# Seeding a PSUM bank from VectorE: beta1 h + bias is written ahead of the matmuls of z, in blocks 11 to 22 of a sparse gated graph layer

## The chip, the cores and the metric

The kernel runs on one core of a Trainium2 chip. The metric is device time in microseconds. Before the change the median of three runs is 1075.63 us (1071.70 to 1077.29).

## The reference, cut to what matters

For 16 batches of 1024 nodes with 256 features, an adjacency of 1024 x 1024 with few non-zeros per column, and gates from a two-layer network:

```python
pre_u = einsum('bud,dk->buk', h, W1[:d]);  pre_v = einsum('bvd,dk->bvk', h, W1[d:])
hidden = relu(pre_u[:, :, None, :] + pre_v[:, None, :, :] + b1)
S = sigmoid(einsum('buvk,ko->buvo', hidden, W2)[..., 0] + b2[0])
a_t = einsum('buv,bud->bvd', S * A, h)
m_t = einsum('uv,bud->bvd', A, h) * h
z = beta1 * h + beta2 * (a_t @ Wa + ba) + beta3 * (m_t @ Wm + bm)
```

The last line is the one that the change touches. The kernel scales Wa by beta2 and Wm by beta3 once, and keeps `bias` = beta2 ba + beta3 bm as one row, so that z = beta1 h + bias + a_t Wa + m_t Wm.

## The kernel before, in words

**Blocks and steps.** The output is cut into 32 blocks: a group `g` of four batches and a tile `vt` of 128 target nodes. A block k takes ten steps, n = 10 k + s with s from 0 to 9. A step handles 128 edge slots. GpSimd gathers for them the rows `fetched` (source features and their products with W1) from a table in DRAM, up to eight steps ahead. TensorE spreads the targets' part over the slots (`expand`, L615, into the tile `pc`, two of them), VectorE adds it (`add`, L648), then does relu, the product with W2 and the sum over features in one instruction for each batch (`gate`, L656, four in a step). ScalarE takes the sigmoid (L659) and scales the left operands with it (L661), and TensorE aggregates (L673) into two accumulators, for two steps at a time, in odd steps.

**Work around the steps.** Spread over the ten steps of block k, written out by hand in `products(n, k, s)`, are:
- `rows` (L445 with w_u, then L461 on ScalarE): products for the table of a later group, in the range around the change at s = 2 and s = 8, up to step 222;
- `halves` (s = 1 and 3): the product with w_v for the next block, in two halves. Each takes a bank, starts with a row of b1 (`add_row`, L449), has eight matmuls (L445), and is read by ScalarE twice, into `X` (L482) and `low` (L483). VectorE then subtracts `X` from `low` (L484);
- `turn_over` (s = 8, 9, then 0 and 2 of the next block): four transposes (L691) of the copied accumulator `ev` (L681), a copy into `LT` (L694), and a product with h on VectorE (L705);
- `block_end` (s = 4 to 7, for the block before): z in two halves h = 0, 1 of two batches each. A half starts with the row of bias (`add_row`, L449), has eight matmuls with w_a and eight with w_m (L722), is copied out of PSUM by ScalarE (L736), and has beta1 h added by VectorE one step later (L737), which leaves z in `h_blk`. A DMA from SP's queue writes it (L739). In the last eight blocks, a matmul with beta1 times the identity takes the place of the addition for h = 1 (L726, L728).

**Order.** All engines' instructions stand in the program in the order in which this loop issues them; an engine runs its own in that order. `after(step, f)` puts work off to the end of a later step, behind that step's `gate`.

**The two small banks.** `small()` hands out the PSUM banks for rows, halves, transposes and z: a pool of two (`psm`), taken in turn. Who takes a bank waits until its last reader is done, which is ScalarE's copy. From s = 3 the turn is: half 1 of `halves` (bank X), z's first half (Y), z's second half (X), rows at s = 8 (Y), transposes (X), and so on.

`LISTS` is step 110 and `LAST` step 230. The lists of edges that need VectorE and GpSimd (`lists`, with the tile `few`, L335, L338) are made before step 110.

Of the kernel before, what the change touches and what calls it, by code (L numbers as in the profile page):

```python
# [7 lines left out]
FP = mybir.dt.float32  # L8
FR = mybir.dt.float32r
I32 = mybir.dt.int32  # L10
AF = mybir.ActivationFunctionType
ALU = mybir.AluOpType
AX = mybir.AxisListType
P = 128
# [3 lines left out]
def kernel(  # L18
# [42 lines left out]
    nc = tc.nc  # L61
    B, N, D = x.shape
    NT = N // P
    DC = D // P
    GB = 4
    NG = B // GB
# [4 lines left out]
    E = TW * P  # L71
# [17 lines left out]
    def load_rows(src, n, name, engine=nc.scalar, at_=None):  # L89
        t = const.tile([P, n], FP, name=name) if at_ is None else at_  # L90
        engine.dma_start(t, bass.AP(tensor=src.tensor, offset=src.offset, ap=[[0, P], [1, n]]))
        return t
# [8 lines left out]
    def fixed(shape, name, dt=FP):  # L101
        return const.tile(shape, dt, name=name)
# [9 lines left out]
    upto = fixed([P, E], "upto")  # L112
# [3 lines left out]
    row = rows32[:, 0:1]  # L116
# [62 lines left out]
    slot, nth = upto, upto[:, :S]  # L179


    unit = fixed([P, P], "unit", FR)
    nc.vector.tensor_scalar(unit, upto[:, :P], 0.0, None, ALU.is_ge)
    edge = fixed([P, 1], "edge")
    nc.vector.tensor_scalar(edge, inw, 0.0, None, ALU.is_equal)

# [6 lines left out]
    bias_p = fixed([P, D], "bias_p", FR)  # L193
# [12 lines left out]
    main = ctx.enter_context(ExitStack())  # L206
# [6 lines left out]
    lst = ExitStack()  # L213
    lists_done = lst.close
    lst = lst.enter_context(tc.tile_pool(name="lst", bufs=1))
    psc = main.enter_context(tc.tile_pool(name="psc", bufs=2, space=bass.MemoryType.PSUM))
    psa = main.enter_context(tc.tile_pool(name="psa", bufs=1, space=bass.MemoryType.PSUM))
    psm = main.enter_context(tc.tile_pool(name="psm", bufs=2, space=bass.MemoryType.PSUM))

    def small(name):  # L220
        return psm.tile([P, 512], FP, name="misc")


    def aside(vt):
# [17 lines left out]
    def lists(vt):  # L242
# [7 lines left out]
        for c in range(0, N, N if vt < EARLY else N // 2):  # L250
            c = slice(c, c + (N if vt < EARLY else N // 2))
# [36 lines left out]
        for i in range(4):  # L288
            nc.tensor.matmul(pw[:, i:i + 1], sums[:, i].rearrange("p w q v -> p (w q v)"), R[:, 0:1],
                             start=True, stop=True)  # L290
# [36 lines left out]
        nc.vector.tensor_tensor(thr[:, vt:vt + 1], last, none, ALU.add)  # L327
        yield "op"
        RR = lst.tile([P, NW, RC], FP, name="RR", bufs=2)
        few = lst.tile([P, E], mybir.dt.uint8, name="few", bufs=2)  # L330
        yield "slot"
        for w, mine in enumerate((soon, late)):
            nc.vector.tensor_scalar(RR[:, w, :], R, mine, None, ALU.mult)
# [68 lines left out]
    def after(step, f):  # L402
        due.setdefault(step, []).append(f)
# [41 lines left out]
                nc.tensor.matmul(p[:, bb * D:(bb + 1) * D], hT[:, 2 * h + bb, i, :], wt[:, i, :],  # L445
                                 start=(i == 0 and not begun), stop=(i == DC - 1), skip_group_check=begun)

    def add_row(p, parts):
        nc.tensor.matmul(p, unit, parts.unsqueeze(1).to_broadcast([P, 2, D]),  # L449
                         start=True, stop=False, skip_group_check=True)  # L450

    def rows(k, tab=None):

# [14 lines left out]

    cuts = {}

    def halves(k):
        X = cuts[k] = big.tile([P, NW, GD], FR, name="X")
        low = one.tile([P, GD], FP, name="low")
        for h in range(2):
            step = yield
            c = slice(2 * h * D, (2 * h + 2) * D)
            p = small("p")
            add_row(p, b1_p)  # L480
            half_product(p, hTs[order[k]], w_v, h, True)
            nc.scalar.copy(X[:, 0, c], p)  # L482
            nc.scalar.copy(low[:, c], p)  # L483
        after(step + (2 if k else 1), lambda: nc.vector.tensor_tensor(low, low, X[:, 0, :].bitcast(FP), ALU.subtract))  # L484
        yield
        nc.scalar.copy(X[W:, 1, :], X[W:, 0, :].bitcast(FP))
        for w in range(NW):
            yield
            nc.scalar.copy(X[(1 - w) * W:(2 - w) * W, w, :], low[w * W:(w + 1) * W])  # L489
# [46 lines left out]
    spare = spare_.rearrange("p b c n -> p b (c n)")  # L536
# [9 lines left out]
    marks, pcs, accs, evs, hbs, LTs, lefts = {}, {}, {}, {}, {}, {}, {}  # L546
# [12 lines left out]
    parts = halves(0)  # L559
    for t, turns_ in enumerate(script):  # L560
        step = t - 100
# [148 lines left out]
    def block_end(k):  # L710

        g, vt = order[k]
        hb = hbs[k]
        for h in range(2):
            for i, wt in ((1, w_a), (0, w_m)):
                step = yield
                if i:
                    pz = small("pz")
                    add_row(pz, bias_p)
                for bb in range(2):  # L720
                    for c in range(DC):
                        nc.tensor.matmul(pz[:, bb * D:(bb + 1) * D], LTs[k][:, 2 * h + bb, i if bb else 1 - i, c, :], wt[:, c, :],  # L722
                                         start=False, stop=(i == 0 and c == DC - 1), skip_group_check=True)
            if h == 1 and g == NG - 1:
                for bb in range(2):
                    nc.tensor.matmul(pz[:, bb * D:(bb + 1) * D], be1_eye[0], hb[h][:, bb, :], start=False, stop=True,  # L726
                                     skip_group_check=True)
                nc.scalar.copy(hb[h], pz.rearrange("p (b d) -> p b d", b=2))  # L728
                b = g * GB + 2 * h
                after(step + 2, lambda hb=hb[h], b=b: nc.sync.dma_start(  # L730
                    out[b:b + 2, vt * P:(vt + 1) * P, :].rearrange("b p d -> p b d"), hb))
                continue
            z = pz.rearrange("p (b d) -> p b d", b=2)
            if step >= ROOM:
                z = LTs[k][:, 2 * h].rearrange("p k c n -> p (k c n)").rearrange("p (b d) -> p b d", b=2)
                nc.scalar.copy(z, pz.rearrange("p (b d) -> p b d", b=2))  # L736
            after(step + 1, lambda hb=hb[h], z=z: nc.vector.scalar_tensor_tensor(hb, hb, be1, z, ALU.mult, ALU.add))  # L737
            b = g * GB + 2 * h
            after(step + 2, lambda hb=hb[h], b=b: nc.sync.dma_start(  # L739
                out[b:b + 2, vt * P:(vt + 1) * P, :].rearrange("b p d -> p b d"), hb))  # L740
        del hbs[k], LTs[k]
# [120 lines left out]
    ROOM, MORE, LISTS = 10, 3, 110  # L862
    LAST = (BS - NT - 1) * T
# [18 lines left out]
    for n in range(total + 2):  # L882
        k, s = divmod(n, T)
        if n < total - 3:
            last_in = n - 1 if n % 2 or n < ROOM else done
        else:
            last_in = n
        while done < min(last_in, total):
            gather_in(done)
            done += 1  # L890
        if n % TW == 1 and n // TW + 1 < total // TW:
            load_mark(n // TW + 1)
        if n < LAST:
            expand(n + 2)
            if n >= ROOM:
                fill(n, False)
            products(n, k, s)
        if n + 1 < total:
            add(n + 1)
        if n < total:  # L900
            gate(n)
            if n + 1 < total:
                left_adj(n + 1)
        do(n)
        if s == 8 and ROOM <= n < LAST:
            turn_over(k, 0, 0, n)
        if n >= LAST and n + 2 < total:
            expand(n + 2)
        if n == 1:
            bias = load_rows(bm, D, "bias", nc.sync, spare[:, 1])  # L910
            ba_b = load_rows(ba, D, "ba_b", nc.sync, spare[:, 2])
            be1 = load_rows(beta1, 1, "be1", nc.sync)
            be2 = load_rows(beta2, 1, "be2", nc.sync)
            be3 = load_rows(beta3, 1, "be3", nc.sync)
            after(10, scale_late)
        if s in (5, 7) and k < BS - 1:
            h = s // 7
            hb = big.tile([P, 2, D], FP, name="h_blk", bufs=4)
            hbs.setdefault(k, []).append(hb)
            g, vt = order[k]  # L920
            nc.sync.dma_start(hb.rearrange("p b d -> p (b d)"),
                              table[g][vt * P:(vt + 1) * P, GD + 2 * h * D:GD + (2 * h + 2) * D])
        if n == total - 6:
            hbs[BS - 1] = hT_free.pop(0).rearrange("p b c n -> p b (c n)")
            for v, m, f in tails:
                for h, o in tail_rows(x, v, m, f):
                    nc.sync.dma_start(h, o)
        for i in advance.get(n, ()):
            next(made[i], None)
        if n in start_list:  # L930
            running.append([made[start_list[n]], True, n])
            piece_of(running[-1], n)
        if n < ROOM or n >= LAST:
            fill(n, False)
        if n >= LAST:
            products(n, k, s)
        if n == LISTS:
            assert not running and all(next(x, None) is None for x in made)
            lists_done()
            more = main.enter_context(tc.tile_pool(name="more", bufs=1))  # L940
            hT_free.extend(hT_places(more, MORE, NH))
            be1_eye.append(more.tile([P, P], FP, name="be1_eye"))
            nc.vector.tensor_scalar(be1_eye[0], ident, be1, None, ALU.mult)
        if n == 120:
            nc.gpsimd.partition_all_reduce(longest, rest, P, bass_isa.ReduceOp.max)
            after(n + 12, count_rest)
# [115 lines left out]
```

## Time and profile before

| | before |
|---|---|
| median of three runs | 1075.63 us (1071.70 to 1077.29) |
| the profiled execution | 1082.24 us, its span 1080.4 us |
| TensorE (PE) busy | 1020.1 us (94%) |
| VectorE (DVE) busy | 1017.6 us (94%) |
| ScalarE (ACT) busy | 862.6 us (80%) |
| GpSimd (POOL) busy | 459.3 us (43%) |
| granted TensorE clock | 0.99 in the mean |
| row of bias or b1 (L449) | 126 matmuls, 411 ns (b1) and 397 ns (bias) each |
| beta1 h added by VectorE (L737) | 55 instructions, 744 ns each |

How to read it: a time in the profile is that of one instruction from its start to its end. Neighbouring instructions of one engine overlap at their ends, so what an instruction takes of its engine is the distance from its start to the next one's start. PE and PEld are TensorE's matmuls and its weight loads; a load runs beside the matmul before it.

### The profile page before, as it was taken

How to read it: one execution, taken by the hardware profiler on the slowest of the kernel's cores; microseconds unless marked ns; L12 is line 12 of the kernel's file. 1: busy time of each engine (PE TensorE's matmuls, PEld its weight loads, DVE VectorE, ACT ScalarE, POOL GpSimd, SP SyncE). 2: the span in 40 equal slices, each digit the busy share in tenths (PEclk: the TensorE clock that was granted, in tenths of full speed). 3: DMA queues.
4: the chain of work that ended last, by engine and by line, in shares of the span. 5: the costliest groups of instructions: out<-in, count | busy, mean ns of one | idle time of the engine just before them, and what ended most of it. 6: DMA issues, size and time to landing. Idle time of an engine off the chain costs nothing.

```text
span 1080.4 us, 24120 instructions
## 1 busy us (share of the span) xinstructions
PE 1020.1 (94%) x7673; PEld 731.3 (68%) x7673; DVE 1017.6 (94%) x3481; ACT 862.6 (80%) x2616; POOL 459.3 (43%) x456
## 2 busy tenths in 40 slices
PE   7777999999999999999999999999999999999996
PEld 6654676776666776677777767777766667666654
DVE  8687999998999999999999999999999999999993
ACT  3246787788888887898888888889889889999983
POOL 2666676555257334553333334333333333333330
PEclk9989999999999999999999999999999999999999
DMA  9999899999999999999999999999999999999991
GB/s 283 327 340 385 313 339 381 362 382 378 403 352 371 408 381 385 379 403 395 404 393 399 412 384 392 408 396 389 381 361 370 369 348 368 365 381 369 365 341 44
DMA packets 147752, 394.56 MB, mean 365 GB/s; under 512 B 18224, under 2 KB 94512, under 8 KB 111408
## 3 DMA queue, kind: packets, MB, share of 16 engines
q0 software_dynamic: 50544, 301.16, 70.9%
q1 hardware_dynamic: 83776, 78.66, 22.9%
q10 hardware_dynamic: 13296, 13.11, 3.5%
q8 instruction: 63, 1.03, 0.4%
q14 instruction: 73, 0.60, 0.1%
HBM read 396.93 MB, written 50.33 MB: 414 GB/s over the span
## 4 chain that ended last, share of the span: by engine, by line
PE 40%; DVE 34%; issue 10%; ACT 8%; DMA 5%; POOL 2%; another core or an unknown queue 0%; POOLq 0%; DVEq 0%; ACTq 0%
DVE fetched L656 16%; DVE fetched L648 12%; PE acc L673 10%; PE misc L722 10%; PE misc L445 9%; PE pc L615 7%; DMA fetched<-table,uidx 3%; PE misc L691 2%; ACT left L661 2%; DVE LT L705 1%; ACT X L489 1%; PE misc L449 1%; DVE low L484 1%; DVE h_blk L737 1%; DMA hT__635<-in_xT_dram 1%
## 5 line engine op out<-in xcount | busy, mean ns | idle before, releaser
L518 POOL DMA_INDIRECT fetched<-table,uidx x320 | 339.4, 1061 | 529.0 <-PE acc L673 389.0
L656 DVE SCALAR_TENSOR_TENSOR fetched<-fetched,w_b 128x256 f32<-128x256 f32 x1280 | 478.0, 419 | 0.0
L648 DVE TENSOR_TENSOR fetched<-fetched,pc 128x1024 f32<-128x1024 f32 x320 | 387.7, 1212 | 29.9 <-PE pc L615 19.4
L661 ACT ACTIVATE left<-left,gt 128x32 f32<-128x32 f32 (+1 forms) x1280 | 299.6, 305 | 10.4
L673 PE MATMUL acc<-fetched,left 128*32 128x256 f32 x4096 | 273.4, 385 | 6.3 <-ACT gt L659 3.7
L615 PE MATMUL pc<-X,mark 128*128 128x512 f32 x640 | 243.7, 462 | 10.9 <-DVE fetched L648 9.3
L673 PEld LDWEIGHTS acc<-fetched,left 128*32 128x32 f32 x4096 | 127.6, 109 | 112.1 <-issue 29.1
L615 PEld LDWEIGHTS pc<-X,mark 128*128 128x128 f32 x640 | 105.4, 189 | 88.9 <-issue 41.6
L659 ACT ACTIVATE gt<-sc,b_b 128x4 f32<-128x4 f32 x320 | 95.9, 300 | 46.7 <-DVE fetched L656 37.5
L722 PE MATMUL misc<-w_m,LT 128*128 128x256 f32 x496 | 117.3, 379 | 0.0
L722 PE MATMUL misc<-w_a,LT 128*128 128x256 f32 x496 | 117.2, 379 | 0.0
L445 PE MATMUL misc<-w_v,hT 128*128 128x256 f32 x448 | 107.6, 383 | 0.0
L722 PEld LDWEIGHTS misc<-w_a,LT 128*128 128x128 f32 x496 | 93.8, 189 | 15.3 <-issue 0.4
L722 PEld LDWEIGHTS misc<-w_m,LT 128*128 128x128 f32 x496 | 93.8, 190 | 15.1
L625 ACT ACTIVATE left<-onehot,val 128x64 f32<-128x64 bf16 (+1 forms) x320 | 102.9, 322 | 0.0
L385 POOL DMA_INDIRECT val<-in_adjT_dram,vidx x80 | 87.2, 1090 | 34.4 <-issue 20.4
L656 DVE DVE_READ_ACCUMULATOR fetched<-fetched,w_b 128x1 f32 x1280 | 100.7, 79 | 0.0
L691 PE MATMUL misc<-ident,ev 128*128 128x128 f32 x512 | 79.5, 278 | 18.5 <-issue 7.0
L445 PEld LDWEIGHTS misc<-w_v,hT 128*128 128x128 f32 x448 | 86.4, 193 | 14.3
L691 PEld LDWEIGHTS misc<-ident,ev 128*128 128x128 f32 x512 | 60.7, 141 | 45.7 <-ACT ev L681 15.2
L482 ACT CAST X<-misc 128x512 fp32r<-128x512 f32 x64 | 37.1, 580 | 55.2 <-PE misc L445 48.0
L445 PE MATMUL misc<-w_u,hT 128*128 128x256 f32 x320 | 76.6, 386 | 4.0 <-issue 3.8
(185 smaller groups left out, 1011.3 us busy)
## 6 DMA issues: line engine op xcount, KB each, us to landing
h_blk<-table SPq DMA_DIRECT2D x62, 256.0 KB
out_dram<-h_blk SPq DMA_DIRECT2D x62, 256.0 KB
hT<-in_xT_dram SPq DMA_DIRECT2D x28, 512.0 KB
table<-in_x_dram ACTq DMA_DIRECT2D x24, 512.0 KB
table<-tab SPq DMA_DIRECT2D x48, 256.0 KB
fetched<-table,uidx POOLq DMA_INDIRECT x320
table<-in_x_dram SPq DMA_DIRECT2D x8, 512.0 KB
table<-fetched SPq DMA_DIRECT2D x8, 512.0 KB
```

The source lines that it names most:

```text
L385: nc.gpsimd.indirect_dma_start(out=val[:, i, j:j + 1], out_offset=None, in_=adj_flat, in_offset=bass.IndirectOffsetOnAxis(ap=vidx[:, i, j: ...
L445: nc.tensor.matmul(p[:, bb * D:(bb + 1) * D], hT[:, 2 * h + bb, i, :], wt[:, i, :], start=(i == 0 and not begun), stop=(i == DC - 1), skip ...
L518: nc.gpsimd.indirect_dma_start(out=fetched[at_slot[n]], out_offset=None, in_=table[g], in_offset=bass.IndirectOffsetOnAxis(ap=uidx[:, vt * ...
L615: nc.tensor.matmul(pcs[n][:, c], marks[n // TW][:, j * P:(j + 1) * P], cuts[k][:, w, c], start=True, stop=True)
L625: nc.scalar.activation(lefts[n][:, :m, 1::GB, :], onehot[:, i, o:o + m, :].unsqueeze(2).to_broadcast([P, m, GB // 2, V]), AF.Copy, scale=v ...
L648: nc.vector.tensor_tensor(t, t, pcs.pop(n), ALU.add)
L656: nc.vector.scalar_tensor_tensor(t[:, b, :], t[:, b, :], 0.0, w2_b, ALU.max, ALU.mult, accum_out=sc[:, b:b + 1])
L659: nc.scalar.activation(gt, sc, AF.Sigmoid, bias=b2_b)
L661: nc.scalar.activation(lefts[n][:, :m, 2 * b, :], lefts[n][:, :m, 1 + b // 2 * GB, :], AF.Copy, scale=gt[:, b:b + 1])
L673: nc.tensor.matmul(accs[h][b * 2 * V:(b + 1) * 2 * V, r, :], left[:, i, 2 * b - b % 2:2 * b - b % 2 + 2].rearrange("p k v -> p (k v)"), f[ ...
L691: nc.tensor.transpose(pt[:, r, :, c, :], ev[:, r, c * P:(c + 1) * P], ident)
L722: nc.tensor.matmul(pz[:, bb * D:(bb + 1) * D], LTs[k][:, 2 * h + bb, i if bb else 1 - i, c, :], wt[:, c, :], start=False, stop=(i == 0 and ...
```

## The change

For the second half of z (h = 1) of the block that ends during blocks 11 to 22 (steps 113 to 223 carry the call), the bank is claimed earlier and filled by VectorE:

- At s = 3, right after ScalarE's two copies of `halves`' second half, `seed_z` claims the same bank X again. At the end of step s = 4 VectorE writes beta1 h + bias into it.
- At s = 6 `block_end` takes this bank instead of a new one and leaves out the row of bias. Its matmuls add to what is there.
- At s = 7 ScalarE copies the bank into `h_blk` itself, and the addition on VectorE at the end of s = 8 is gone.
- While the bank is kept, `small()` gives out only the other one. The pool of two tiles becomes two named tiles, one each.

Three more edits make room in SBUF for a `bias` that stays: `unit`, the 128 x 128 ones that are the weights of every row of bias or b1, becomes one column read with a step of zero; `few` has one buffer instead of two; `bias` has a tile of its own. The branches for steps from LAST on are not reached, since the call is limited to steps between LISTS and LAST.

```diff
-    unit = fixed([P, P], "unit", FR)
-    nc.vector.tensor_scalar(unit, upto[:, :P], 0.0, None, ALU.is_ge)
+    unit_ = fixed([P, 1], "unit", FR)
+    nc.vector.tensor_scalar(unit_, row, 0.0, None, ALU.is_ge)
+    unit = unit_.to_broadcast([P, P])
...
-    def small(name):
-        return psm.tile([P, 512], FP, name="misc")
+    turn_of, kept = [0], []
+
+    def small(name, bank=None):
+        if bank is None:
+            bank = turn_of[0] = 1 - turn_of[0]
+            if kept and kept[0][0] == bank:
+                bank = turn_of[0] = 1 - bank
+        return psm.tile([P, 512], FP, name=f"misc{bank}")
...
-        few = lst.tile([P, E], mybir.dt.uint8, name="few", bufs=2)
+        few = lst.tile([P, E], mybir.dt.uint8, name="few", bufs=1)
...
-    def add_row(p, parts):
+    def add_row(p, parts, start=True):
         nc.tensor.matmul(p, unit, parts.unsqueeze(1).to_broadcast([P, 2, D]),
-                         start=True, stop=False, skip_group_check=True)
+                         start=start, stop=False, skip_group_check=True)
...
+    def seed_z(k, step):
+        bank = turn_of[0]
+        pz = small("pz", bank)
+        kept.append((bank, pz))
+
+        def write():
+            z, hb = pz.rearrange("p (b d) -> p b d", d=D), hbs[k][1]
+            if step >= LAST:
+                nc.scalar.activation(z, hb, AF.Copy, scale=be1)
+            else:
+                nc.vector.scalar_tensor_tensor(z, hb, be1, bias.unsqueeze(1).to_broadcast([P, 2, D]), ALU.mult, ALU.add)
+        if step >= LAST:
+            write()
+        else:
+            after(step + 1, write)
...
             nc.scalar.copy(low[:, c], p)
+            if h == 1 and k > 1 and (LISTS < step < LAST):
+                seed_z(k - 2, step)
...
                 if i:
-                    pz = small("pz")
-                    add_row(pz, bias_p)
+                    filled = h == 1 and kept
+                    pz = kept.pop()[1] if filled else small("pz")
+                    if not filled or step >= LAST + 6:
+                        add_row(pz, bias_p, not filled)
...
-            if h == 1 and g == NG - 1:
+            by_eye = g == NG - 1 and h == 1
+            if by_eye:
...
+            if by_eye or filled:
                 nc.scalar.copy(hb[h], pz.rearrange("p (b d) -> p b d", b=2))
...
-            z = pz.rearrange("p (b d) -> p b d", b=2)
-            if step >= ROOM:
-                z = LTs[k][:, 2 * h].rearrange("p k c n -> p (k c n)").rearrange("p (b d) -> p b d", b=2)
-                nc.scalar.copy(z, pz.rearrange("p (b d) -> p b d", b=2))
-            after(step + 1, lambda hb=hb[h], z=z: nc.vector.scalar_tensor_tensor(hb, hb, be1, z, ALU.mult, ALU.add))
-            b = g * GB + 2 * h
+            else:
+                z = pz.rearrange("p (b d) -> p b d", b=2)
+                if step >= ROOM:
+                    z = LTs[k][:, 2 * h].rearrange("p k c n -> p (k c n)").rearrange("p (b d) -> p b d", b=2)
+                    nc.scalar.copy(z, pz.rearrange("p (b d) -> p b d", b=2))
+                after(step + 1, lambda hb=hb[h], z=z: nc.vector.scalar_tensor_tensor(hb, hb, be1, z, ALU.mult, ALU.add))
...
-            bias = load_rows(bm, D, "bias", nc.sync, spare[:, 1])
+            bias = load_rows(bm, D, "bias", nc.sync)
```

More of the change, by code (lines that the diff above doesn't have):

```diff
@@ L217 @@
     psa = main.enter_context(tc.tile_pool(name="psa", bufs=1, space=bass.MemoryType.PSUM))
-    psm = main.enter_context(tc.tile_pool(name="psm", bufs=2, space=bass.MemoryType.PSUM))
-    def small(name):
-        return psm.tile([P, 512], FP, name="misc")
+    psm = main.enter_context(tc.tile_pool(name="psm", bufs=1, space=bass.MemoryType.PSUM))
+    turn_of, kept = [0], []
[5 more added lines that the diff above has]
+        return psm.tile([P, 512], FP, name=f"misc{bank}")
     def aside(vt):
@@ L727, in block_end @@
                                      skip_group_check=True)
+            b = g * GB + 2 * h
+            if by_eye or filled:
                 nc.scalar.copy(hb[h], pz.rearrange("p (b d) -> p b d", b=2))
-                b = g * GB + 2 * h
-                after(step + 2, lambda hb=hb[h], b=b: nc.sync.dma_start(
-                    out[b:b + 2, vt * P:(vt + 1) * P, :].rearrange("b p d -> p b d"), hb))
-                continue
-            z = pz.rearrange("p (b d) -> p b d", b=2)
-            if step >= ROOM:
-                z = LTs[k][:, 2 * h].rearrange("p k c n -> p (k c n)").rearrange("p (b d) -> p b d", b=2)
-                nc.scalar.copy(z, pz.rearrange("p (b d) -> p b d", b=2))
-            after(step + 1, lambda hb=hb[h], z=z: nc.vector.scalar_tensor_tensor(hb, hb, be1, z, ALU.mult, ALU.add))
-            b = g * GB + 2 * h
+            else:
[4 more added lines that the diff above has]
+                after(step + 1, lambda hb=hb[h], z=z: nc.vector.scalar_tensor_tensor(hb, hb, be1, z, ALU.mult, ALU.add))
             after(step + 2, lambda hb=hb[h], b=b: nc.sync.dma_start(
```

## The prediction, made before the changed kernel ran

> **What bounds the kernel now.** I read the page first, then the busy times by stage, the groups by form, the chain of waits in one block of the range, and single instructions. A block's ten steps start where VectorE's addition L648 of step 10 k starts: block 12 at 471 us, block 23 at 804 us.
>
> The page's totals, then three stages (columns: length, busy us and instructions of PE, PEld, DVE, ACT, POOL, granted clock, DMA share, GB/s):
>
> ```profile
> span 1080.4 us, 24120 instructions
> PE 1020.1 (94%) x7673; PEld 731.3 (68%) x7673; DVE 1017.6 (94%) x3481; ACT 862.6 (80%) x2616; POOL 459.3 (43%) x456
> ```
>
> ```profile
> 471.00:622.00 151.00, 150.63 (x1164) 109.70 (x1163) 145.80 (x480) 131.92 (x406) 53.07 (x51) 1.00 1.02 402
> 653.00:804.00 151.00, 150.66 (x1176) 109.20 (x1175) 145.05 (x477) 131.97 (x406) 54.05 (x50) 1.00 1.01 388
> 833.00:1060.00 227.00, 218.89 (x1728) 152.88 (x1724) 225.87 (x755) 200.49 (x626) 77.23 (x76) 1.00 0.94 354
> ```
>
> The page cannot tell PE from DVE, both 94%. The stages can: in the change's range PE is busy 150.66 of 151 us and DVE has 6 us free in five blocks, 1.2 us a block; from 833 us on DVE is full. So a saving on PE can count in the range, a saving on DVE cannot. Blocks 12 to 22 take about 30.1 us each.
>
> The forms that the change touches:
>
> ```profile
> L449 PE MATMUL misc<-bias_p,unit 128*128 128x512 f32 x62 | 24.6, 397 | 0.6 <-ACT LT L736 0.6
> L737 DVE SCALAR_TENSOR_TENSOR h_blk<-h_blk,be,LT 128x512 f32<-128x512 f32 x55 | 40.9, 744 | 0.0
> L774 DVE SCALAR_TENSOR_TENSOR hT<-hT,be,misc 128x512 f32<-128x512 f32 x1 | 0.7, 747 | 0.8 <-PE misc L767 0.8
> ```
>
> And the chain through s = 7 of block 19 to s = 0 of block 20 (start, us, what):
>
> ```profile
> 706.67 0.23 PE misc L449
> 706.91 1.73 PE misc L722 x8
> ...
> 710.29 1.74 PE misc L722 x8
> 712.06 0.59 ACT LT L736
> 712.67 1.05 ACT X L489
> ...
> 717.61 0.49 ACT ev L681
> 718.09 0.04 issue
> 718.14 0.66 PE misc L691 x4
> ```
>
> The row of bias is on the chain, but with 0.23 us, not its 0.40: the rest overlaps the next matmul. After L722 the chain leaves PE: ScalarE runs 6.0 us without a break from the copy of z to the copy `ev`, for which the transposes at s = 0 wait. PE's own work in between (rows, transposes, aggregates, expansions) ends only a little sooner. In the single records the pair of expansions ahead has its second matmul at 717.67; with 0.23 us for it and 0.11 for each transpose the fourth would start at 718.23, and it starts at 718.52. So PE has 0.29 us to spare there, once a block.
>
> **The change, part by part.** The row of bias is left out 12 times on PE at s = 6: 12 x 0.23 = 2.8 us less. ScalarE can follow: its copy before L736 starts at 741.48 in block 20, such copies follow each other by 0.48 us, so L736 can start at 741.96, which is 0.23 before its 742.19.
>
> The bank's new neighbour costs. Half 2 of z keeps bank X from s = 3, the first half takes Y, and no other bank is given out until s = 8. There rows take "the other one than Y", which is X: the bank that ScalarE has just begun to copy. Before, rows took Y, free since s = 5. The trace shows both cases; the upper lines are from an earlier block where lists had shifted the turn, the lower ones from block 20:
>
> ```profile
> 402.59 0.82 PE L615 MATMUL pc<-X,mark 128*128 128x512 f32 x2
> 402.98 0.59 ACT L736 COPY LT<-misc 128x512 f32<-128x512 f32 x1 [0.67 <-PE misc L722]
> 403.59 1.04 ACT L489 CAST X<-low 64x1024 fp32r<-64x1024 f32 x1
> 403.61 0.73 PEld L445 LDWEIGHTS misc<-w_u,hT 128*128 128x128 f32 x4 [0.65 <-ACT LT L736]
> ```
>
> ```profile
> 741.80 0.81 PE L615 MATMUL pc<-X,mark 128*128 128x512 f32 x2
> 742.19 0.59 ACT L736 COPY LT<-misc 128x512 f32<-128x512 f32 x1
> 742.22 1.71 PEld L445 LDWEIGHTS misc<-w_u,hT 128*128 128x128 f32 x8
> 742.45 1.89 PE L445 MATMUL misc<-w_u,hT 128*128 128x256 f32 x8
> ```
>
> In the lower case the second matmul of the rows starts 0.45 us after the second expansion, in the upper case 0.93 us: a stall of 0.48 us. Rows stand at s = 8 in blocks 11 to 21 (the last at step 218), 11 times: 5.3 us more. Of each, 0.29 us goes into the slack at the transposes, if ScalarE's chain moves ahead with the saving: 11 x 0.29 = 3.2 us back.
>
> Here a rule speaks against the change. "Perfetto Trace Analysis", section Matmuls, says that independent groups of matmuls should rotate through the banks, so that the emptying of one overlaps the next group. Taken alone it would charge each stall in full, and the sum would be +2.5 us instead of -0.7.
>
> On VectorE an instruction of 744 ns (0.66 us from start to start) moves from the end of s = 8 to the end of s = 4, of the same operation and size. Its target is now PSUM, which no VectorE row shows. Bounds: L774, which reads PSUM, takes 747 ns against 744 with all in SBUF, so 3 ns; at the far end the same again, 0.66 us; and it could be shorter by what the write to SBUF costs, at most the 0.2 us by which 744 ns exceeds 512 elements at the 1.04 ns each that L774's two forms (256 and 512 wide, 481 and 747 ns) show. I take 0, by the nearest row. Even +0.66 us fits into the 1.2 us that VectorE has free in each block. "Perfetto Trace Analysis", section Optimizing Scalar/DVE Operations, gives VectorE about 60 ns of access for SBUF and 125 for PSUM: that would make 12 x 0.065 = 0.8 us, hidden too; the rows for reading do not agree.
>
> New waits. VectorE's write waits for ScalarE's copy `low` of s = 3. It ends 0.3 to 0.7 us before gate 4 does in ten of the 12 blocks, and 0.5 and 0.35 us after it in blocks 11 and 17: 0.8 us in all, and behind it stand only L648 and the gates of s = 5 to 8, which ScalarE takes up 2.7 us or more after they end. Nothing on the chain. The expansions of s = 6 to 9 that follow these additions start at least 2.6 us after the addition that they need, so a delay of 0.66 us reaches no one; the cover is this lead. TensorE's wait for the write at s = 6 is over by 5 us. The write needs `h_blk` 13 us sooner than the addition did: block 19's second half is issued by 712.0, the packets of SP's queue taken in order put its landing at 716.3, and the write comes at 731. Nothing.
>
> Moved besides: the output's DMA stays at s = 9 behind the same neighbours in SP's queue. `few` with one buffer: the second copy starts at 42.2 us when the first's packets had landed at 29.2, the third at 52.5 after 50.1, the later ones later still, so GpSimd's queue waits for nothing. `bias` in its own tile: no new work. `unit` read with step zero is the weight of 114 rows; no load with step zero is in the trace. The present load takes 188 ns and lies beside the matmul before it, which holds PE 0.23 us, so up to 0.23 us it is free. I take 188, the same count of elements; below that there is nothing to gain, since it is hidden; twice as long, it shows 0.376 - 0.232 = 0.144 us.
>
> The sum against the profiled run: 1082.24 - 2.8 + 5.3 - 3.2 = 1081.5 us, that is -0.7. The profiled run is 6.6 us above the median, so I put the same -0.7 on 1075.63: **1074.9 us**. A measurement here tells about 0.5%, 5.4 us, from no change, so this is no difference.
>
> **The rivals.**
> - The stall is absorbed in full, or the rows do not wait: -12 x 0.23 = -2.8, 1072.9 us. For it: ScalarE has 0.16 us idle ahead of L736 in block 19, so its copy could come that much sooner still if TensorE let it. Against: the slack of 0.29 is less than 0.48, and the stall is seen at 403.6.
> - The stall is not absorbed, because ScalarE's chain does not move ahead or PE is late again before the transposes: +5.3 - 2.8 = +2.5, 1078.1 us.
> - Faster beyond doubt: the addition at the end of s = 8 stands in front of all VectorE work of the next block, and if it held the chain, its move to s = 4 would give 12 x 0.67 = 8.0 us, 1067.6 us. Against: VectorE waits 1.1 to 1.2 us for PE at s = 1 in these blocks, behind this very addition.
> - Slower: the weight load with step zero. Its place is each row of b1 or bias, its price 0.144 us if the load doubles, and it decides once the load is longer than 0.232 us. In blocks 12 to 22, where PE is full, 33 such rows stand: +4.8 us, 1079.7 with the -0.7; if all 114 rows counted, +16 us, about 1091. If the load tripled it would be 11 us in these blocks alone. Against: it reads as many elements as before.
>
> **How the numbers follow.** The forecast 0.44, full gain 0.12, full stall 0.12: all within 0.5%, together 0.68. VectorE's relief 0.12 is the chance of faster. The slow load 0.20 is the chance of slower. The range reaches from below the full gain, by half of the spread of the three runs' lower side (1075.6 - 1071.7 = 3.9, so 1072.9 - 1.9 = 1071.0), up over the full stall and over the doubled load in the full blocks (1079.7) to 1081.0. It leaves out the relief and the larger part of the slow load that is over that, and none of the rest. The three cases within 0.5% alone would have 1072.9 to 1078.1.
>
> **What would show it.** In the profile after: 50 rows of bias instead of 62; 43 instructions of L737's kind into `h_blk`, and 12 of them into a bank, of about 744 ns; 11 waits of the rows at s = 8 for ScalarE's copy, with 0.6 us of idle weight load each; the wait of the transposes at s = 0 for `ev` gone or under 0.1 us in these blocks; blocks of 30.0 to 30.1 us as before. I am wrong if the blocks 12 to 21 change by more than 0.3 us each, if L449's load is longer than 232 ns, or if blocks outside the range change.

## The result, and the profile after

The changed kernel took 1086.09 us in the median (1082.35 to 1090.32), the kernel before on the same chip 1076.75 us (1071.70 to 1080.40). The ratio is 1.0089, with a 95% interval from 1.0060 to 1.0119: slower by 9.6 us (6.5 to 12.8). The forecast was no difference, with 1081.0 us as the upper end of its range. The profiled execution took 1085.9 us for 1082.24 before, a smaller difference than that of the medians: this one execution reached the first block 4.1 us sooner (62.1 for 66.3 us), ahead of all that the seeds and the lists' bank touch.

Three views of the profile after are read in the order of the prediction: the totals, the forms that the change touches, and the waits.

The totals (busy time, share of the span, instructions):

```profile
span 1084.0 us, 24142 instructions
PE 1021.3 (94%) x7673; PEld 733.5 (68%) x7673; DVE 1027.2 (95%) x3493; ACT 862.7 (80%) x2616; POOL 464.1 (43%) x456
```

TensorE has 7673 matmuls, the same number as before. Twelve rows of bias left out would have made 7661. VectorE has 12 instructions more, 3493 for 3481, where a moved instruction would have left the number alone. Nothing was taken away. The forms say the same (instruction, count, then busy us and mean ns of one, then idle time before it):

```profile
L455 PE MATMUL misc<-bias_p,unit 128*128 128x512 f32 x62 | 24.7, 399 | 0.4 <-ACT LT L762 0.4
L455 PEld LDWEIGHTS misc<-bias_p,unit 128*128 128x128 f32 x62 | 11.6, 187 | 3.8 <-ACT LT L762 1.3
L763 DVE SCALAR_TENSOR_TENSOR h_blk<-h_blk,be,LT 128x512 f32<-128x512 f32 x55 | 41.3, 750 | 0.2 <-DMA h_blk<-table 0.2
...
L487 DVE SCALAR_TENSOR_TENSOR misc<-h_blk,be,bias 128x512 f32<-128x512 f32 x12 | 9.2, 764 | 3.8 <-DMA h_blk<-table 3.8
```

All 62 rows of bias and all 55 additions are still there. VectorE's 12 writes (L487) have come on top, and one of them waited 3.8 us for its `h_blk`. So the bank is filled and then overwritten. The reason is in the code: `filled = h == 1 and kept` makes `filled` the list `kept` itself, not a yes or no. The next line, `kept.pop()`, empties that list, and `not filled` two lines on is then true. The row of bias starts the bank anew, and the old way with ScalarE's copy and VectorE's addition follows.

The second reading is further from the change. These are the waits of TensorE's weight loads from 150 to 450 us, blocks 2 to 10, which lie ahead of every fill. After:

```profile
PEld misc L451 <- DVE from L306: 8.9, 2, 5.6
PEld acc L697 <- issue: 8.5, 39, 0.3
PEld misc L715 <- DVE from L306: 5.6, 1, 5.6
```

L306 is the last of four small reads by which VectorE takes the tile `pw` of the lists out of its bank (L300 before). Rows of the table (L451) and transposes (L715) wait for it three times, 14.5 us in all. In the same view of before there is one such wait, of 1.0 us:

```profile
PEld misc L691 <- DVE from L300: 1.0, 1, 1.0
```

In the timeline of TensorE's loads after, the first of the three looks so (start, us, engine, line, with the idle time before it in brackets):

```profile
177.08 1.09 PEld L295 LDWEIGHTS misc<-R,sums 128*128 128x128 f32 x8
...
179.94 0.41 PEld L639 LDWEIGHTS pc<-X,mark 128*128 128x128 f32 x2
185.95 3.06 PEld L451 LDWEIGHTS misc<-w_u,hT__1792 128*128 128x128 f32 x8 [5.61 <-DVE from L306]
```

At 177.08 TensorE fills `pw`. The rows that it should begin at 180.3 get the same bank, and VectorE, in whose order additions and gates stand between the four reads, ends the fourth at 185.90. For VectorE, what comes behind this wait is worse than the wait. In stretches of time (length, then busy us and instructions of PE, PEld, DVE, ACT and POOL, granted clock, DMA share, GB/s), first of after, then of before, there with the whole stage:

```profile
180.00:186.00 6.00, 0.83 (x5) 0.37 (x3) 6.00 (x24) 2.53 (x9) 1.57 (x2) 0.88 1.04 395
186.00:191.00 5.00, 5.00 (x20) 3.62 (x24) 0.24 (x2) 0.96 (x2) 0.00 (x0) 0.50 0.35 122
```

```profile
180.00:186.00 6.00, 6.00 (x49) 4.50 (x47) 6.00 (x26) 4.71 (x16) 4.07 (x4) 1.00 1.00 369
186.00:191.00 5.00, 2.33 (x10) 1.44 (x8) 5.00 (x19) 2.90 (x9) 3.16 (x3) 1.00 1.04 398
...
140.00:440.00 300.00, 288.36 (x2177) 207.27 (x2180) 292.94 (x1024) 244.58 (x742) 149.69 (x149) 1.00 1.02 379
```

TensorE was busy 0.83 of 6 us, then ran 5 us at a granted clock of 0.50. VectorE still had work during the wait (6.00 of 6.00); in the 5 us behind it, it worked 0.24 us. VectorE is nearly full in this stage before (292.94 of 300 us), so it can hardly make up for what it loses. Block 3, in which all this falls, took 39.90 us, for 35.20 before.

Why do these waits exist? The banks that `small()` gave out in the built programs, one digit for each tile (6 and 7 are the two banks), for the same 70 tiles of both, around the lists:

```
before  6767677676767676767676767777676767676767676767676767677776767767676767
after   6767676767676767676767676767676767676767676767676767676767676767676767
```

The pool of two did not take turns. Where `pw` was held, it gave out the other bank up to four times in a row. The two named tiles do take turns, and so hand the held bank to TensorE.

### The profile page after: what moved, and what is told of

Same layout as the page of the kernel before. It is cut to its first block, busy times and chain, and to the rows that moved or that the text cites. A ratio compares the mean times of both kernels' runs of the same rounds, so it can differ in the third digit from the quotient of the medians.

```text
span 1084.0 us, 24142 instructions
## 1 busy us (share of the span) xinstructions
PE 1021.3 (94%) x7673; PEld 733.5 (68%) x7673; DVE 1027.2 (95%) x3493; ACT 862.7 (80%) x2616; POOL 464.1 (43%) x456
## 4 chain that ended last, share of the span: by engine, by line
PE 52%; DVE 33%; DMA 6%; issue 5%; ACT 4%; SPq 0%; POOL 0%; ACTq 0%; DVEq 0%; POOLq 0%
PE misc L451 14%; DVE fetched L680 14%; PE acc L697 12%; DVE fetched L672 12%; PE misc L748 11%; PE pc L639 8%; PE misc L715 3%; DMA table<-tab 2%; PE misc L455 2%; DMA hT<-in_xT_dram 1%; DVE LT L729 1%; DVE low L508 1%; DVE h_blk L763 1%; ACT left L685 1%; DMA fetched<-table,uidx 1%
## 5 line engine op out<-in xcount | busy, mean ns | idle before, releaser
L542 POOL DMA_INDIRECT fetched<-table,uidx x320 | 343.2, 1072 | 528.2 <-PE acc L697 330.1
L680 DVE DVE_READ_ACCUMULATOR fetched<-fetched,w_b 128x1 f32 x1280 | 110.1, 86 | 0.0
L451 PE MATMUL misc<-w_v,hT 128*128 128x256 f32 x448 | 107.5, 383 | 0.0
L451 PEld LDWEIGHTS misc<-w_v,hT 128*128 128x128 f32 x448 | 86.1, 192 | 14.0
L715 PE MATMUL misc<-ident,ev 128*128 128x128 f32 x512 | 80.2, 280 | 13.9 <-ACT ev L705 7.1
L715 PEld LDWEIGHTS misc<-ident,ev 128*128 128x128 f32 x512 | 62.8, 144 | 38.1 <-ACT ev L705 15.8
L451 PE MATMUL misc<-w_u,hT 128*128 128x256 f32 x320 | 76.2, 386 | 4.6 <-DVE from L306 2.9
## 6 DMA issues: line engine op xcount, KB each, us to landing
h_blk<-table SPq DMA_DIRECT2D x62, 256.0 KB, 11.5
table<-tab SPq DMA_DIRECT2D x48, 256.0 KB, 12.7
```

The source lines that it names most:

```text
L542: nc.gpsimd.indirect_dma_start(out=fetched[at_slot[n]], out_offset=None, in_=table[g], in_offset=bass.IndirectOffsetOnAxis(ap=uidx[:, vt * ...
L680: nc.vector.scalar_tensor_tensor(t[:, b, :], t[:, b, :], 0.0, w2_b, ALU.max, ALU.mult, accum_out=sc[:, b:b + 1])
L715: nc.tensor.transpose(pt[:, r, :, c, :], ev[:, r, c * P:(c + 1) * P], ident)
```

## The experiments

Theory A: the loss lies mostly outside the range, in the strict turn of the two banks; in the range, the unused fill costs a little and saves nothing. Theory B: it lies in the range, with the 12 writes and the rows at s = 8. Theory C: the three edits for room cost. All ratios are against runs of the kernel before on the same chip (its median was 1088.21 us beside the strict turn alone, the edits for room, the change with its fill used, and pool back with the fill used; 1083.31 us beside the turn that passes over the lists' bank, the change without a fill, pool back with the fill unused, and the load earlier; 1083.22 us beside the two rows left out).

**The strict turn alone** (the kernel before with one edit):

```diff
-    psm = main.enter_context(tc.tile_pool(name="psm", bufs=2, space=bass.MemoryType.PSUM))
+    psm = main.enter_context(tc.tile_pool(name="psm", bufs=1, space=bass.MemoryType.PSUM))
+    turn_of = [0]
     def small(name):
-        return psm.tile([P, 512], FP, name="misc")
+        turn_of[0] = 1 - turn_of[0]
+        return psm.tile([P, 512], FP, name=f"misc{turn_of[0]}")
```

> The kernel before with one edit: the two small banks are two named tiles in strict turn instead of a pool of two. Nothing is seeded, no row of bias is left out. Theory A (the time is lost outside the range, where TensorE now waits for VectorE's reads of a bank that the lists hold): slower by 5 to 8 us, ratio 1.005 to 1.008; idle stretches of TensorE of about 5.6, 5.6 and 3.3 us ended by VectorE's small reads in blocks 3, 6 and 10, the granted clock at 0.5 for several us right behind them, blocks 11 to 22 as before within 0.5 us in all. Theory B (the time is lost in blocks 11 to 22, by the 12 extra writes of VectorE and the rows at s = 8 that wait for ScalarE): no change, ratio 0.999 to 1.001, since neither is in this kernel.

Measured: 1094.89 us, ratio 1.0063 (1.0038 to 1.0088), that is 6.9 us slower (4.1 to 9.6). The waits are there (L302 is the last read of `pw` here), and so is the clock, in the 5 us behind the wait in block 6:

```profile
PEld misc L447 <- DVE from L302: 6.6, 2, 3.4
PEld misc L693 <- DVE from L302: 5.6, 1, 5.6
```

```profile
299.00:304.00 5.00, 4.88 (x34) 3.12 (x34) 3.28 (x15) 3.66 (x14) 0.00 (x0) 0.51 0.77 313
```

Theory B expected no change, and it falls as the explanation of the main part.

**The edits for room alone** (`unit` read with step zero, `few` with one buffer, `bias` in its own tile; the diff is that of the change).

> The kernel before with the three edits that make room alone: the weights of every row of bias or b1 read with step zero, few with one buffer, bias in its own tile. Theory A: no change, ratio 0.999 to 1.001, the weight load of the rows stays at 187 to 190 ns. Theory C (these edits, through GpSimd's waits for the one buffer or the moved addresses, make a part of the loss): slower by 3 us or more, ratio 1.003 and up, with TensorE idle in the blocks of the lists.

Measured: ratio 0.9992 (0.9965 to 1.0018). The weight load of a row of bias takes 187 ns for 188 before, that of a row of b1 192 ns in both. Theory C falls, and with it the prediction's rival of the slow weight load.

**The strict turn, but passing over the lists' bank.** `held_` holds the bank of `pw` from its matmuls to the fourth read:

```diff
     def small(name):
         turn_of[0] = 1 - turn_of[0]
+        if turn_of[0] in held_:
+            turn_of[0] = 1 - turn_of[0]
...
         pw = aside(vt)
+        if vt >= EARLY - 1:
+            held_.append(turn_of[0])
...
         nc.vector.tensor_tensor(from_, pw[:, 3:4], from_, ALU.max)
+        held_.clear()
```

> The kernel before with the two named banks in strict turn, but a bank is passed over while VectorE still has to read it for the lists (the tile pw, from its matmuls to its last of four reads). Theory A (it is this one bank that TensorE waits for): back at the time of before, ratio 0.998 to 1.002, blocks 6 to 10 together at 162 us instead of the 166.7 of the strict turn, no idle stretch of TensorE of 2.5 us or more that is ended by a read of pw. Theory D (the strict turn costs by other waits, of TensorE for ScalarE's copies in general, which a pool evades too): ratio 1.004 to 1.007, blocks 6 to 10 stay near 166 us.

Measured: 1083.71 us, ratio 0.9990 (0.9963 to 1.0017). Blocks 6 to 10 take 161.7 us, as before, where the strict turn takes 166.6. Of the waits for `pw`'s last read (L307 here) two are left, 1.0 and 0.3 us long. The loss of the strict turn is this one bank, and no other wait that a pool evades.

**The change without a fill** (the condition for `seed_z` set to `False`; strict turn and room remain).

> The changed kernel without any fill: the strict turn and the three edits for room remain. Theory A (turn): as slow as the strict turn alone, ratio 1.004 to 1.008, blocks 16 to 22 at 30.1 us, and 2 to 5 us below the changed kernel. Theory B (fill): no change against before, ratio 0.999 to 1.001.

Measured: ratio 1.0075 (1.0043 to 1.0107), 8.1 us slower. Against the 9.6 us of the change, what the fills add is too small to tell from totals; the blocks below tell it.

**The change with its fill used:**

```diff
-                    filled = h == 1 and kept
+                    filled = h == 1 and bool(kept)
```

> The changed kernel with the flag taken as a value before the list is emptied, so that the filled bank is really used: 12 rows of bias and 12 additions fewer, the strict turn and the wait of the rows at s = 8 stay. Theory A: blocks 11 to 22 lose the 0.15 us a block that the changed kernel shows and end 0.04 us a block below before (30.08 us), so some 2.3 us less than the changed kernel; what is outside the range stays, so slower than before by 4.5 to 7.5 us, ratio 1.004 to 1.007. Theory B (the unused fill, with its row of bias and second addition, makes the whole loss): level with before, ratio 0.998 to 1.001.

Measured: ratio 1.0086 (1.0055 to 1.0117), 9.4 us slower. Now the counts are those of the prediction:

```profile
L763 DVE SCALAR_TENSOR_TENSOR h_blk<-h_blk,be,LT 128x512 f32<-128x512 f32 x43 | 32.1, 747 | 0.2 <-ACT LT L762 0.2
...
L455 PE MATMUL misc<-bias_p,unit 128*128 128x512 f32 x50 | 20.0, 400 | 0.4 <-ACT LT L762 0.4
...
L487 DVE SCALAR_TENSOR_TENSOR misc<-h_blk,be,bias 128x512 f32<-128x512 f32 x12 | 9.1, 756 | 2.0 <-PE acc L697 1.6 <-ACT left L685 0.3
```

Blocks 18 to 22 take 30.04 us for 30.27 in the change, 0.23 us less, the price of a row as the prediction had it. That the whole would be some 2.3 us faster than the change was expected and is not shown: the interval, 6.0 to 12.7 us, holds both 7.5, the upper end of what was expected, and 9.6 us. In this profile blocks 0 to 5 took 221.6 us, where those of kernels with the pool of two lie between 213.2 and 221.3. Theory B's number (level with before) is excluded.

**The change with the pool of two back, the fill still unused.** The filled tile is the one of `halves`' second half, kept alive, so that the pool passes it over by itself (the lines of `psm` and `small` are those of before again):

```diff
-    def seed_z(k, step):
-        bank = turn_of[0]
-        pz = small("pz", bank)
-        kept.append((bank, pz))
+    def seed_z(k, step, pz):
+        kept.append((0, pz))
...
-                seed_z(k - 2, step)
+                seed_z(k - 2, step, p)
```

> The changed kernel with the pool of two restored and the flag as it is there: the bank is filled by VectorE 12 times, and then the row of bias overwrites it and the addition follows. It shows what the unused fill costs without the strict turn. Theory A (VectorE has room for 12 x 0.66 us, and what costs is only a late h_blk): blocks 12 to 22 that do not wait for h_blk at 30.1 us, up to three that wait 3 to 4 us; ratio 1.000 to 1.004. Theory B (the writes themselves fall on the path): +0.66 us for each, 12 x 0.66 = 8 us, ratio 1.006 to 1.008, blocks 12 to 22 near 30.8 us.

Measured: ratio 1.0028 (0.9996 to 1.0061). Blocks 20 to 22 take 30.09 us, so the writes themselves are covered. Block 13, at 32.23 us, and 14 and 16, at 31.31 and 32.04, are late, and before VectorE's writes 6.8 us of idle time stand in three pieces of 1.7 to 2.5 us and one of 0.3. The profile puts these down to engines; the next two runs bear on what it is.

**Pool back and fill used** (the two edits together).

> The idea alone: the pool of two as before, the filled bank is the tile of the halves' second half itself, held until z's second half is done, and the fill is used (50 rows of bias). The rows at s = 8 then take the bank of z's first half, free since s = 5. Theory A: no wait of the rows for ScalarE, no wait for the lists' bank; 12 x 0.23 = 2.8 us less on TensorE in the range: faster by 1.5 to 3.5 us, ratio 0.9967 to 0.9986, blocks 12 to 22 at 29.9 us. Theory B (the write of VectorE into the bank costs more than the row that it saves): slower by 1 us or more, ratio over 1.001, with blocks 12 to 22 longer than 30.15 us.

Measured: 1087.00 us, ratio 0.9989 (0.9966 to 1.0011). Blocks 18 to 22 take 29.94 us, 0.20 below before. But the write (L482 here) still stands idle in two blocks:

```profile
L482 DVE SCALAR_TENSOR_TENSOR misc<-h_blk,be,bias 128x512 f32<-128x512 f32 x12 | 9.1, 759 | 6.9 <-ACT left L680 3.6 <-DMA h_blk<-table 3.3
```

Of the 6.9 us, 3.3 are put down to the load of `h_blk` (block 13, which takes 33.47 us) and another 3.3 to ScalarE's `left` (block 16, 33.27 us). The write reads no `left`, and ScalarE's copy of the bank that it does need had ended 3.8 us earlier. That leaves `h_blk` there too; the next run tests it.

**The load earlier.** In the blocks concerned, `h_blk` of the second half is loaded first:

```diff
-            h = s // 7
+            h = s // 7 if k < 10 or k > 21 else 1 - s // 7
             hb = big.tile([P, 2, D], FP, name="h_blk", bufs=4)
-            hbs.setdefault(k, []).append(hb)
+            hbs.setdefault(k, {})[h] = hb
```

> The idea with the pool of two and the fill used, as in the run before of that name, and one edit more: for the blocks whose second half is filled, h_blk of the second half is loaded at s = 5 and that of the first half at s = 7, instead of the other way round, so the filled half's h has 6 us more to land. Theory A (VectorE's write waits for h_blk because the write comes four steps sooner than the addition did): no wait of the write for h_blk, no block of 12 to 22 over 31 us, these blocks at 29.9 us in the mean; faster than before by 2 to 4 us, ratio 0.9963 to 0.9982. Theory E (the load is late because SP's queue is held for 10 us and more by full transfers, whatever it stands behind): waits of 3 us stay in one to three blocks, ratio 0.998 to 1.000.

Measured: 1082.88 us, ratio 0.9988 (0.9953 to 1.0023). VectorE's waits from 450 to 810 us:

```profile
DVE fetched L667 <- PE pc L634: 11.1, 14, 1.2
DVE h_blk L758 <- DMA h_blk<-table: 0.9, 2, 0.7
DVE LT L724 <- issue: 0.5, 1, 0.5
DVE misc L482 <- ACT low L500: 0.4, 1, 0.4
```

The write waits for no load any more; the addition of the first half (L758), whose load now comes second, does so twice, for 0.9 us in all. What stays for the write is 0.4 us for ScalarE's copy `low`, which the prediction had (0.5 and 0.35 us in two blocks). No block from 12 to 22 is over 30.7 us, and those from 18 to 22 take 29.97. The gain in the total that was expected, 2 to 4 us, is inside the interval but not shown.

**A second row left out.** The same for z's first half, in the bank of the transposes of s = 2, written at the end of s = 3. This kernel does not compute the z of the reference, and why stays open; the run stands for its time alone.

```diff
+        if w == 1 and q == 1 and LISTS < step < LAST:
+            seed_z(k, step, pt_, 0)
...
-                    filled = h == 1 and bool(kept)
+                    filled = h in kept
```

> The version with the pool of two, the fill used and the earlier load, taken one step further: z's first half is filled too, in blocks 11 to 22. Its bank is that of the transposes of s = 2, VectorE writes beta1 h + bias there at the end of s = 3, and both halves of h_blk are loaded at s = 5. 38 rows of bias and 31 additions are left. Theory A (TensorE bounds these blocks, so each row left out counts with nearly its 0.23 us): blocks 18 to 22 at 29.75 us in the mean, against 29.95 with one row left out and 30.13 before; in all 3 to 5 us below before, ratio 0.9954 to 0.9972. Theory F (ScalarE's and VectorE's chain is next, and a further row buys nothing): these blocks stay at 29.9 to 30.0 us, ratio 0.998 to 1.000; a write that waits for h_blk would show as VectorE's idle time of 3 us in single blocks.

Measured: ratio 1.0005 (0.9979 to 1.0031). Blocks 18 to 22 take 29.81 us, another 0.16 less, so the row does count there. The total shows nothing of it: block 15 alone took 34.53 us, and new waits for transfers stand in the range:

```profile
ACT tab L464 <- DMA table<-tab: 3.2, 2, 2.9
DVE fetched L667 <- DMA fetched<-table,uidx: 2.6, 3, 1.0
```

The wait of 2.9 us is in block 15. Behind it TensorE stood idle for 1.65 and 1.22 us, and its granted clock was 0.50 for the next 5 us:

```profile
563.00:567.00 4.00, 1.49 (x8) 1.06 (x9) 3.96 (x13) 3.32 (x11) 0.99 (x1) 0.84 1.06 394
567.00:572.00 5.00, 5.00 (x32) 2.66 (x31) 2.00 (x10) 4.39 (x16) 1.78 (x2) 0.50 0.99 398
```

The blocks of all profiles, from the starts of VectorE's addition in step 10 k (us; one profile each, so single blocks differ by chance, and blocks 0 to 5 by up to 10 us together):

| | 0 to 5 | 6 to 10 | 11 to 23 | 24 to 30 | mean of 18 to 22 |
|---|---|---|---|---|---|
| before | 213.2 | 161.7 | 392.5 | 198.1 | 30.13 |
| room alone | 215.0 | 162.2 | 394.2 | 198.1 | 30.11 |
| turn that passes the held bank | 216.0 | 161.7 | 392.1 | 198.0 | 30.15 |
| the change | 214.4 | 166.6 | 394.1 | 198.0 | 30.27 |
| strict turn alone | 223.9 | 166.6 | 391.2 | 198.2 | 30.17 |
| change without a fill | 217.2 | 169.0 | 391.7 | 198.0 | 30.10 |
| change, fill used | 221.6 | 167.0 | 393.0 | 198.1 | 30.04 |
| pool, fill unused | 214.4 | 161.6 | 394.3 | 198.0 | 29.94 (20 to 22: 30.09) |
| pool, fill used | 221.3 | 162.8 | 393.6 | 198.1 | 29.94 |
| the same, load earlier | 213.9 | 161.6 | 390.5 | 198.0 | 29.97 |
| two rows left out | 214.9 | 161.5 | 392.3 | 198.0 | 29.81 |

The column of blocks 6 to 10 is the clearest: all four kernels with the strict turn stand at 166.6 to 169.0 us, all seven others at 161.5 to 162.8. The column on the right orders the kernels by what TensorE does in the range.

## Why the prediction was wrong, point by point

**The step that failed most: "The pool of two tiles becomes two named tiles, one each", taken as no change.** The text on the banks read the pool as strict turn ("taken in turn"), and the sum held no term for it. Alone it costs 6.9 us (4.1 to 9.6), where the whole change costs 9.6. The prediction even had the hint in hand: it showed a place at 402.6 us "where lists had shifted the turn", and used it as a precedent for a stall without asking what had shifted it. The condition it set itself, "I am wrong if blocks outside the range change", is what happened, by 4.9 us in blocks 6 to 10 and by 4.7 us in block 3 (the sum of blocks 0 to 5 hides the latter, since block 1 was 4.1 us shorter in that execution).

**"The row of bias is left out 12 times": it is not.** The term of -2.8 us was 0 in the change, because the flag is an alias of the emptied list. That the change doesn't do what it says was no rival in the prediction, and two lines of the diff were enough to see it. The size of the term was right: used, the fill takes 0.23 us from each of the blocks 18 to 22 (30.27 to 30.04).

**"The write needs h_blk 13 us sooner ... Nothing": it is not nothing.** The landing was worked out for block 19 alone, and 716.3 against 731 us looked like much. In the change one write waited 3.8 us, which blocks 13 and 14 together show as 2.8 us more than before (63.12 for 60.28). With the pool back and the fill used, two writes waited 3.3 us each. The prediction's own stages showed DMA shares of 1.02 and 1.01 in the range, and the loads of `h_blk` do not land alike there: in the profile after they land between 11.5 and 25.5 us after the start of their issue (from 490 to 760 us, where the trace has the landing), while the 716.3 of the prediction is 7.9 us after it. For block 19 even 11.6 us were early enough. In the timeline of SP's queue of after, the issue of the load that came late took 7.67 us; its data landed at 524.12, 25.5 us after the start, and on VectorE the write, due at 520.4, began only at 524.25:

```profile
498.66 7.67 SPq L946 DMA_DIRECT2D h_blk<-table  x1
```

```profile
524.25 0.76 DVE L487 SCALAR_TENSOR_TENSOR misc<-h_blk,be,bias 128x512 f32<-128x512 f32 x1 [3.80 <-DMA h_blk<-table]
```

The same load took as long to issue before (8.73 us at 496.30), but there its data had until the addition, four steps later.

**What held: the stall of the rows and its absorption.** +0.48 - 0.29 = +0.19 us a block was expected for the wait at s = 8 alone. The change, which has that wait and no saving, shows +0.14 (30.27 for 30.13). Its timeline in block 19 has the wait as foreseen, and right behind it the transposes (L715) with no wait for `ev` any more:

```profile
715.19 0.59 ACT L762 COPY LT<-misc 128x512 f32<-128x512 f32 x1 [0.16 <-PE misc L748]
...
715.83 1.59 PEld L451 LDWEIGHTS misc<-w_u,hT 128*128 128x128 f32 x8 [0.65 <-ACT LT L762]
715.83 1.99 PE L451 MATMUL misc<-w_u,hT 128*128 128x256 f32 x8 [0.21 <-ACT LT L762]
...
717.44 0.58 PEld L715 LDWEIGHTS misc<-ident,ev 128*128 128x128 f32 x4
```

The matmuls themselves stood idle for 0.21 us of the 0.65 that the weight load waited. The same in blocks 18 to 22 together, first before, with five waits for `ev`, then after, where these are gone and five waits for the copy (L762) stand in their place:

```profile
PEld misc L691 <- ACT ev L681: 2.5, 5, 0.5
...
PEld misc L451 <- ACT LT L762: 2.6, 4, 0.6
PEld misc L715 <- ACT LT L762: 0.6, 1, 0.6
```

With the fill used, -0.04 a block was expected, and -0.09 came.

**What held: the rest at nothing.** The weights with step zero (187 ns), `few` and `bias` cost nothing (0.9992), and VectorE's write into a bank takes 764 ns for 744, inside its bounds, and is covered by the idle time of VectorE, which falls from 1.19 to 0.67 us a block in blocks 18 to 22.

**Of the rivals none was right.** The case of slower by over 0.5% did come, but through the bank, not through the weight load that the prediction gave it to. The full gain is what the idea is worth at best: without the wait at s = 8 (pool back), 0.16 to 0.20 us of the 0.23 are seen in blocks 18 to 22, which for 12 blocks would be 1.9 to 2.4 us, an estimate. That is too little for the totals (0.9989 and 0.9988, with intervals that hold 1). Two rows give 0.32 us a block and no shown gain in the total. In the one profile of that kernel the range lost its gain in block 15, to a wait for a transfer and the low clock behind it; that this is so in every run was not shown. No kernel here is shown to beat the one before.

## What to carry to other kernels

When an edit replaces a pool by named buffers, compare the sequence of buffers that both programs give out over the whole kernel, not just where the edit aims: a pool that skips what is held hides waits that a fixed turn brings back. Before costing what a diff removes, follow its flags once by hand, and keep the rival that it removes nothing. Where an instruction is moved ahead of its operand's old deadline, check the landing in every block of the range, the more so where the DMA share is at 1.

## What the runs showed of the hardware that was not expected

A few microseconds without matmuls cost more than themselves. After 5.2 us in which TensorE was idle in the stretch before 186 us, the granted clock was 0.50 for the next 5 us; after 2.9 us of idle time before 405.5 us it was 0.57 in the mean of the next four:

```profile
402.00:406.00 4.00, 1.14 (x5) 0.66 (x4) 3.78 (x18) 3.12 (x8) 0.50 (x1) 1.00 1.07 357
406.00:410.00 4.00, 4.00 (x23) 2.75 (x25) 3.68 (x14) 0.00 (x0) 0.00 (x0) 0.57 1.01 398
```

Not each such gap did it. The gap before 405.5 us, in block 10, stands in all four kernels with the strict turn, 2.8 to 2.9 us long. Behind it the clock fell in two of them, the change and the change without a fill (first line below), and stayed at 1.00 in the other two, the strict turn alone (second line) and the change with its fill used:

```profile
412.12:416.12 4.00, 4.00 (x12) 3.09 (x12) 3.91 (x16) 0.28 (x1) 0.00 (x0) 0.57 0.91 363
...
424.63:428.63 4.00, 4.00 (x44) 2.88 (x44) 3.90 (x16) 1.94 (x8) 0.27 (x1) 1.00 0.98 393
```

The eight matmuls of the rows, with which TensorE starts again, took 3.68 us in the first of these and 1.99 in the second:

```profile
412.12 3.68 PE L451 MATMUL misc<-w_u,hT 128*128 128x256 f32 x8 [2.84 <-DVE from L306]
...
424.63 1.99 PE L447 MATMUL misc<-w_u,hT 128*128 128x256 f32 x8 [2.83 <-DVE from L302]
```

Block 10 took 36.49 and 36.74 us in the first two kernels, 34.85 and 34.86 in the other two, and 34.01 before. So the wait cost 0.8 us there, and the fall of the clock another 1.6 to 1.9, by one profile of each. What tells the two pairs apart stays open.

The clock also falls without the strict turn: in block 15 with two rows left out, as shown above, and with the pool back and the fill used, where it was 0.51 from 191 to 198 us, in a block 3 that took 41.65 us. So a long block in a single profile need not be the doing of the edit.
